# A two-layer graph network on one core: the second batch's preparation regrouped around the first output product

## The chip, the core and the metric

The kernel runs on one core of a Trainium2 chip. The metric is device time in microseconds (us) of one launch. Five engines work side by side, each through its own instructions in program order: TensorE (PE in the profile, with its weight loads as PEld), VectorE (DVE), ScalarE (ACT), GpSimd (POOL) and SyncE (SP), which here issues nearly all DMAs.

## The reference

32 graphs ("batches") of 512 nodes with 512 features pass through two layers. All arithmetic is in fp32.

```python
# layer 0
h = relu(layernorm(x))
agg = (adj @ h) / max(rowsum(adj), 1e-6)
x = x + relu(concat([h, agg], -1) @ W.T)
# layer 1
h = relu(layernorm(x))
q, k = split(h @ Wqk);  v = h @ Wv
w = scale * mask * rowsum(q * (adj @ (k * mask)))
x = x + softmax(w, over the nodes)[:, None] * v
```

## The kernel before

**Products.** Every 512x512 product is computed in seven block products instead of eight, from left and right sums of the operand's quarter blocks. An operand therefore sits in SBUF as seven "slots" of 128 x 512 fp32: the four quarters in slots 0 to 3, and sums of them in slots 4 to 6. `left_sums` and `right_sums` are four VectorE instructions each that fill in slots 4, 6, 5 and rewrite slot 2 (left) or slot 1 (right). `product` (L112) runs through the blocks in the order 1, 2, 6, 5, 7, 3, 4, or with `sooner` 1, 2, 5, 6, 7, 3, 4. Blocks 1, 6, 7 and 4 accumulate in one PSUM tile (`pp`), which ScalarE copies out after each of them (the copies `c11`, `c12`, `c22`), so a block on `pp` can't begin before the copy of the one before it is done.

**Order.** A batch b goes through four products: `layer0_y` (Y: h times the second half of W), `layer0_out` (O: h times the first half, plus adjacency times Y, 14 steps of 8 matmuls), `layer1_tv` (TV, 28 half steps of matmuls, run as 14 steps) and `layer1_u` (U: adjacency times the masked h of layer 1). Y and U have 7 steps of 8 matmuls. The order in time is Y(0), O(0), Y(1), U(0), O(1), TV(0), U(1), Y(2), O(2), and so on. Letters with a batch number are used in this way below.

**Steps.** The program order is written by hand. `run` (L165) advances a product by one step and then emits whatever the `Plan` holds for this step, so an entry `p.at(5, f)` puts f's instructions behind those of step 5 on every engine that they use. A product's copies of a finished block are emitted when the next step begins: in O, `c11` stands at the start of step 2, the DVE work on the first quarter at that of step 4, `c12` at that of step 6, the copy of block 5 at that of step 8, and `c22` at that of step 10. In Y(1), `c11` stands at step 1, the copy of block 5 at 3, `c12` at 4 and `c22` at 5.

**Front work.** While a batch is multiplied, the next ones are prepared:

- `FrontH` (L290) makes h of layer 0: `load` reads x in two halves (8 DMAs of 128 KB), `stats` takes mean and variance of a chunk of 128 rows on VectorE, `variance` forms 1/sqrt on VectorE and GpSimd, `shift` its product with the mean, `write` normalizes a chunk on ScalarE and writes it to DRAM scratch `dhT` (256 KB), `to.read` reads it back with rows and columns exchanged in blocks (4 DMAs of 128 KB a half, tile `shT`), and `turn` transposes a half on VectorE into slots 0, 1 or 2, 3.
- `FrontA` (L317) does this for the adjacency: `load`, `sum` (row sums on ScalarE), `degrees` (VectorE), `write` (scaled by 1/degree on ScalarE, to `daT`), `to.read` (tile `saT`), `turn`.
- `FrontH1` (L357) makes h of layer 1 from the x that O leaves, with `mask` and `masked_sums` for U's right operand and `sh1T` for its transpose; `keep` stores x (1 MB, `dx`).
- `Stream` (L404) reads the seven slots of W's first half ("W1") from DRAM scratch `dw`, 256 KB each, for each O from O(1) on, with four buffers.

In `start` (L778) W1 lies in SBUF as `w1R`, in one half of the tile `tv`, whose other half holds `HT[1]`, the transposed h of batch 1. `w1R` is copied to `dw` for later use, and after O(0) its space becomes Y(1)'s output. The adjacency of batches 0 and 1 uses one tile, `aT`. The half tiles that x and adj are loaded into (tag "n") have two buffers, as have the tiles for the exchanged reads (tag "s").

Of the kernel before, what the change touches and what calls it, by code (L numbers as in the profile page):

```python
# [22 lines left out]
def kernel(  # L23
# [11 lines left out]
    nc = tc.nc  # L35
# [25 lines left out]
    def slots(tag, bufs, name, pool=None):  # L61
        return (pool or big).tile([P, 7, 2, H], F32, tag=tag, bufs=bufs, name=name)
# [19 lines left out]
    def left_sums(s, on=None):  # L82

        return [
            lambda: add(s(4), s(2), s(3), on), lambda: sub(s(6), s(0), s(2), on),
            lambda: sub(s(5), s(4), s(0), on), lambda: sub(s(2), s(1), s(5), on),
        ]
# [7 lines left out]
    def of(t):  # L95
        return lambda i: t[:, i]
# [15 lines left out]
    def product(name, terms, place, finish, seed=False, sooner=False):  # L112

        def m(k, p, first):
            for n, (lt, rt) in enumerate(terms):
                block_product(k, p, lt, rt, first and n == 0)  # L120
                yield

        pp = mm_tile(f"pp_{name}")
        yield from m(1, pp, True)
        if seed:
            pr = seed_tile(f"pr_{name}")
            copy(pr, pp)
            pq = mm_tile(f"pq_{name}")
            yield from m(5, pq, True)
            m5 = block(f"m5_{name}")  # L130
            copy(m5, pq)
            yield from m(6, pp, False)
            c12 = place(0, 1)
            copy(c12, pp)
            yield from m(2, pr, False)
            finish(0, 0, None, pr, None)
        else:
            c11 = place(0, 0)
            copy(c11, pp)
            pr = mm_tile(f"pr_{name}")  # L140
            yield from m(2, pr, True)
            finish(0, 0, c11, pr, c11)
            for k in (5, 6) if sooner else (6, 5):
                if k == 6:
                    yield from m(6, pp, False)
                    c12 = place(0, 1)
                    copy(c12, pp)
                else:
                    pq = mm_tile(f"pq_{name}")
                    yield from m(5, pq, True)  # L150
                    m5 = block(f"m5_{name}")
                    copy(m5, pq)
        yield from m(7, pp, False)
        c22 = place(1, 1)
        copy(c22, pp)
        finish(1, 1, c22, m5, c22)
        yield from m(3, pq, False)
        finish(0, 1, c12, pq, c12)
        yield from m(4, pp, False)
        finish(1, 0, None, pp, None)  # L160

    def right(t):
        return lambda k: t[:, RIGHT[k]]

    def run(phase, n, plan):  # L165

        for i in range(n):
            if phase is not None:
                next(phase)
            for f in plan.get(i, []):  # L170
                f()
        if phase is not None:
            assert next(phase, "end") == "end"
# [79 lines left out]
    def shift(t, a=0, b=C):  # L253
        mv, rstd, nmr = t
        nc.vector.scalar_tensor_tensor(
            nmr[:, a:b], mv[:, a:b, 0], -1.0, rstd[:, a:b], op0=ALU.mult, op1=ALU.mult
        )
# [166 lines left out]
    def into(t):  # L424


        def finish(r, c, o, p, s):
            if s is None:
                copy(t[:, 2 * r + c, :, :], p)
            else:  # L430
                add(o, p, s)

        return (lambda r, c: t[:, 2 * r + c, :, :]), finish

    def layer0_y(b):
        if b not in Y:
            Y[b] = slots("yh", 1, f"y_{b}")
        return product(f"y_{b}", [(HT.get(b, hT), right(w2R))], *into(Y[b]), sooner=b < 2)
# [332 lines left out]
    FH, FA, F1 = {}, {}, {}  # L771
    stream = Stream()
# [5 lines left out]
    def start():  # L778
# [10 lines left out]
        w1R = spread[:, 0:3584].rearrange("p (s b f) -> p s b f", s=7, b=2)  # L789
# [21 lines left out]
        fh = FH[1] = FrontH(1)  # L811
# [36 lines left out]
        def place(d, which, src):  # L848
            nc.scalar.activation(
                mv[:, 2 * (d // 2):2 * (d // 2) + 2, 2 * (d % 2):2 * (d % 2) + 2, which, :],  # L850
                src.rearrange("p (a b f) -> p a b f", a=2, b=2), AF.Copy, scale=1.0 if which else scale,
            )
# [47 lines left out]
        p = Plan()  # L900
# [52 lines left out]
        fb = FA[1] = FrontA(1)  # L953
        p = Plan()
# [1 line left out]
        p.at(0, turn_chunk, Later(rows, 3), 3, "a")  # L956
        p.at(1, keep_chunk, a0, 3, "a")
        p.at(1, fb.load, 0)
        p.at(2, fb.load, 1)
        la = left_sums(of(a0))  # L960
        for k in range(4):
            p.at(2 + k // 2, la[k])
        for c in range(C):
            p.at(2 + c, fh.stats, c)
            p.at(6 + c // 2, fh.write, c)
        p.at(5, variance, fh.t)
        p[6].insert(0, lambda: shift(fh.t))
        p.at(7, lambda: nc.sync.dma_start(out=stream.d.rearrange("s p b f -> p s (b f)"), in_=w1R.rearrange("p s b f -> p s (b f)")))
        p.at(7, mask_order)
        p.at(8, mask_turn)  # L970
        p.at(9, mask_keep)
        p.at(8, fh.to.read, 0)
        p.at(9, fh.to.read, 1)
        for c in range(C):
            p.at(8 + c, lambda c=c: place(c, 1, wvN[:, c, :]))
            p.at(10 + c, fb.sum, c)
        p.at(10, fh.turn, 0)
        p.at(11, fh.turn, 1)
        for k in range(4):
# [1 line left out]
        f = F1[0] = FrontH1(0)  # L981
# [10 lines left out]
        p = Plan()  # L992
# [12 lines left out]
        p.at(2, weights[1])  # L1005
        p.at(3, f.mask, 2)
        p.at(3, f.mask, 3)
        for h in range(2):
            p.at(2 + h, fb.degrees, h)
        for k in range(4):  # L1010
            p.at(4, f.masked_sums, k)
        p.at(4, f.to.read, 0)
        p.at(5, f.to.read, 1)
        p.at(5, fb.write, 0)
        p.at(5, fb.write, 1)
        p.at(5, weights[2])
        p.at(6, weights[3])
        run(layer0_y(1), 7, p)

        fh = FH[2] = FrontH(2)  # L1020
        p = Plan()
        p.at(0, fb.write, 2)
        p.at(0, fb.write, 3)
        p.at(0, f.turn, 0)
        p.at(1, f.turn, 1)
        for n in range(4):
            p.at(0, stream.load)
        p.at(1, fb.to.read, 0)
        p.at(2, fh.load, 0)
        p.at(2, fh.load, 1)  # L1030
        p.at(3, fb.to.read, 1)
        p.at(3, load_x, 1)
        p.at(2, FA[0].factor)
        p.at(2, weights[4])
        r1 = right_sums(of(Y[1]))
        p.at(5, r1[0])
        p.at(6, r1[2])
        for c in range(C):
            p.at(3 + c, fh.stats, c)
        p.at(4, fb.turn, 0)  # L1040
        p.at(6, variance, fh.t)
        run(layer1_u(0), 7, p)
        return weights[5:], mv
# [5 lines left out]
    }  # L1049
    with tc.manual_schedule(engines=engines):  # L1050
        weights, mvR = start()
        post = None
        for i in range(1, B):
            more, last = i + 1 < B, i + 1 == B
            f = F1[i] = FrontH1(i)
            p = Plan()
# [44 lines left out]
            if 1 < i and i + 2 < B:  # L1101
                fh = FH[i + 2]
# [23 lines left out]
            p = Plan()  # L1126
# [19 lines left out]
            if i == 1:  # L1146
# [3 lines left out]
                fh = FH[3]  # L1150
# [29 lines left out]
            p = Plan()  # L1180
# [40 lines left out]
            if more:  # L1221
                p = Plan()
                fb = FA[i + 1]
# [24 lines left out]
        p = Plan()  # L1248
# [11 lines left out]
        p = Plan()  # L1260
# [39 lines left out]
```

## Time and profile before

| | us |
|---|---|
| median of three runs | 2289.23 (2286.17, 2289.23, 2289.88) |
| the profiled execution: its time | 2286.77 |
| the profiled execution: its span, first to last instruction | 2284.8 |
| TensorE busy in the span | 2262.3 (99%) |
| VectorE / ScalarE / GpSimd busy | 1912.4 / 1025.0 / 176.6 |
| DMA traffic | 463.68 MB, mean 203 GB/s |

The start in the same execution, by TensorE's own timeline: the products begin at 24.64 (Y(0)), 39.99 (O(0)), 68.34 (Y(1)), 92.68 (U(0)), 104.77 (O(1)) and 137.27 (TV(0)). A step of 8 matmuls takes 1.73 us from its start to the start of the next when nothing is in its way.

Times in a timeline count from the first instruction. A line there gives start, duration, engine, line of the kernel, instruction, out<-in by the program's tile names, form and count; a bracket gives the engine's idle time before it and what ended it. "SPq" is SyncE's issuing of a DMA, not the transfer.

### The profile page before, as it was taken

The page shows a single profiled execution, that of the slowest core. Times are in us where ns is not written, and L with a number is a line of the kernel's source. Part 1 is how long each engine was busy: PE and PEld are TensorE (multiplying, and loading weights), DVE is VectorE, ACT ScalarE, POOL GpSimd, SP SyncE. Part 2 cuts the span into 40 slices and gives each one's busy share as a digit, 9 for nine tenths or more (in the row PEclk, how much of TensorE's full clock was granted, in tenths as well). Part 3 has the DMA queues.
Part 4 walks back from the last instruction along what each step waited for, and adds up shares of the span by engine and source line. Part 5 has one row for each costly group of instructions (what it writes and reads, how often), then busy time and mean ns, then how long its engine had stood idle before and what let it go on. Part 6 is the DMA issues. An engine that isn't in the chain of part 4 may idle for free.

```text
span 2284.8 us, 32852 instructions
## 1 busy us (share of the span) xinstructions
PE 2262.3 (99%) x10526; PEld 1985.8 (87%) x10526; DVE 1912.4 (84%) x3778; ACT 1025.0 (45%) x1895; POOL 176.6 (8%) x261
## 2 busy tenths in 40 slices
PE   9799999999999999999999999999999999999999
PEld 7688888888888888888888888888888888888888
DVE  6698888888888888888888888888888888888776
ACT  4355344454344544444543454443445434444323
POOL 0000000000000000000011000000000010000000
PEclk9899999999999999999999999999999999999999
DMA  8879777878787877788787878787877877887644
GB/s 183 202 212 245 214 191 209 232 203 209 196 202 219 222 202 209 193 204 233 202 214 199 198 208 231 201 212 187 208 223 216 208 200 197 209 231 204 154 128 107
DMA packets 409900, 463.68 MB, mean 203 GB/s; under 512 B 38112, under 2 KB 271584, under 8 KB 405504
## 3 DMA queue, kind: packets, MB, share of 16 engines
q1 hardware_dynamic: 396512, 426.46, 68.7%
q0 software_dynamic: 8928, 32.51, 8.6%
q10 hardware_dynamic: 4288, 2.62, 0.5%
q8 instruction: 83, 1.36, 0.3%
q14 instruction: 89, 0.73, 0.1%
HBM read 293.93 MB, written 167.51 MB: 202 GB/s over the span
## 4 chain that ended last, share of the span: by engine, by line
PE 94%; DMA 3%; DVE 1%; ACT 0%; issue 0%; SPq 0%; POOL 0%; DVEq 0%; ACTq 0%
PE ptv L470 28%; PE pp_o L103 18%; PE pp_u L103 9%; PE pp_y L103 9%; PE pq_o L103 9%; PE pq_u L103 5%; PE pq_y L103 5%; PE pr_o L103 5%; PE pr_u L103 2%; PE pr_y L103 2%; PE pw L521 1%; DMA w<-dw 1%; DMA mv<-in_L_gnn_Wqk_dram 0%; DMA a<-in_adj_dram 0%; DMA mv<-in_L_gnn_W_dram 0%; DMA dw<-tv 0%
## 5 line engine op out<-in xcount | busy, mean ns | idle before, releaser
L470 PE MATMUL ptv<-mv,h1T 128*128 128x256 f32 x2940 | 639.4, 379 | 0.0
L470 PEld LDWEIGHTS ptv<-mv,h1T 128*128 128x128 f32 x2940 | 558.6, 190 | 75.9
L74 DVE TENSOR_TENSOR tv<-tv 128x256 f32<-128x256 f32 (+1 forms) x645 | 321.5, 510 | 13.2 <-ACT tv L80 1.5
L80 ACT ACTIVATE tv<-ptv 128x512 f32<-128x512 f32 (+1 forms) x360 | 185.0, 541 | 262.9 <-PE ptv L470 261.9
L103 PE MATMUL pp_u<-h1m,aT 128*128 128x256 f32 x1024 | 241.9, 379 | 0.0
L103 PE MATMUL pp_y<-wide 128*128 128x256 f32 x992 | 234.4, 379 | 0.7 <-ACT y L80 0.7
L103 PE MATMUL pp_o<-y,aT 128*128 128x256 f32 x992 | 234.4, 379 | 0.0
L103 PE MATMUL pp_o<-w,wide 128*128 128x256 f32 x960 | 226.8, 379 | 0.0
L103 PEld LDWEIGHTS pp_u<-h1m,aT 128*128 128x128 f32 x1024 | 194.5, 190 | 26.4
L103 PEld LDWEIGHTS pp_y<-wide 128*128 128x128 f32 x992 | 188.3, 190 | 26.6 <-ACT y L80 1.1
L103 PEld LDWEIGHTS pp_o<-y,aT 128*128 128x128 f32 x992 | 188.3, 190 | 25.6
L103 PEld LDWEIGHTS pp_o<-w,wide 128*128 128x128 f32 x960 | 182.4, 190 | 24.8
L80 ACT ACTIVATE o<-pp_o 128x512 f32<-128x512 f32 x96 | 57.3, 597 | 296.0 <-PE pp_o L103 296.0
L80 ACT ACTIVATE y<-pp_y 128x512 f32<-128x512 f32 x124 | 74.0, 597 | 233.8 <-PE pp_y L103 233.8
L74 DVE TENSOR_TENSOR tv<-ptv,tv 128x512 f32<-128x512 f32 x240 | 139.7, 613 | 43.0 <-PE ptv L470 39.2
L77 DVE TENSOR_TENSOR h1T<-h1T 128x512 f32<-128x512 f32 (+1 forms) x189 | 163.3, 878 | 1.3
L80 ACT ACTIVATE xu<-pp_u 128x512 f32<-128x512 f32 x127 | 75.8, 597 | 195.2 <-PE pp_u L103 195.2
L251 POOL TENSOR_TENSOR rstd<-rstd,mhalf 128x2 f32<-128x2 f32 (+1 forms) x97 | 80.0, 825 | 665.4 <-DVE rstd L250 665.4
L103 PE MATMUL pq_u<-h1m,aT 128*128 128x256 f32 x512 | 121.0, 379 | 0.0
L74 DVE TENSOR_TENSOR tv<-ptv,m_tv 128x512 f32<-128x512 f32 (+1 forms) x120 | 72.0, 622 | 56.5 <-PE ptv L470 55.4
L103 PE MATMUL pq_y<-wide 128*128 128x256 f32 x496 | 117.3, 379 | 0.0
L103 PE MATMUL pq_o<-y,aT 128*128 128x256 f32 x496 | 117.2, 379 | 0.0
(167 smaller groups left out, 3321.0 us busy)
## 6 DMA issues: line engine op xcount, KB each, us to landing
w<-dw SPq DMA_DIRECT2D x217, 256.0 KB, 4.2
a<-in_adj_dram SPq DMA_DIRECT2D x256, 128.0 KB, 3.1
dx<-xu SPq DMA_DIRECT2D x32, 1024.0 KB, 4.9
sh1T<-dh1T SPq DMA_DIRECT2D x256, 128.0 KB, 3.4
shT<-dhT SPq DMA_DIRECT2D x248, 128.0 KB, 6.1
daT<-a SPq DMA_DIRECT2D x124, 256.0 KB, 3.1
saT<-daT SPq DMA_DIRECT2D x248, 128.0 KB, 3.4
xu<-in_x_dram SPq DMA_DIRECT2D x124, 256.0 KB, 5.4
```

What stands on the lines that cost most here:

```text
L74: (on or nc.vector).tensor_tensor(o, a, b, op=ALU.add)
L77: (on or nc.vector).tensor_tensor(o, a, b, op=ALU.subtract)
L80: nc.scalar.activation(o, i, AF.Copy)
L103: nc.tensor.matmul(p[:, rc, :], lt[:, LEFT[k], dk, ts(rc, P)], right[:, dk, :], start=first and rc == 0 and dk == 0, stop=True, skip_group ...
L251: nc.gpsimd.tensor_tensor(rstd[:, a:b], rstd[:, a:b], mhalf[:, a:b], op=ALU.pow)
L470: nc.tensor.matmul(banks[n][:, :, ts(i, P)], left[:, LEFT[k], LEFT_IN[j], :], mvR[:, RIGHT[k], RIGHT[j], :, :], start=first and i == 0, st ...
L521: nc.tensor.matmul(banks[n][:, ts(i, P)], left[:, LEFT[k], LEFT_IN[j], :], mvR[:, RIGHT[k], RIGHT[j], which, :], start=first and i == 0, s ...
```

## The change

All of it lies in `start`, in the plans of O(0), Y(1) and U(0).

- In O(0), batch 1's four statistics and their variance move from steps 2 to 5 into step 2, with two of the four sums of `aT` put ahead of them and two behind. The four normalizations and their writes move from steps 6 and 7 to step 5, ahead of the copy `c12`, and the exchanged reads from steps 8 and 9 to step 5.
- The copy of W1 to `dw`, one transfer of 1792 KB behind h's writes, becomes seven of 256 KB: slots 0, 1 and 3 ahead of h's writes (step 2), slots 2, 4, 5 and 6 behind h's reads (step 6).
- Batch 1's adjacency is summed, scaled and written within O(0) (steps 6 to 12) instead of being summed there (10 to 13) and scaled and written in Y(1) and U(0). Its second half is loaded at step 1 instead of 2.
- The mask's work moves by one or two steps.
- In Y(1), the exchanged reads of layer 1's h move one step forward, and the first four loads of W1 slots move here from U(0), behind those reads.
- In U(0), the adjacency's exchanged reads come at steps 0 and 1 (before: 1 and 3), x of batch 2 ("the third x") is loaded behind them (before: between the two), the first adjacency transpose moves from step 4 to 3, ahead of the third x's statistics, which move from steps 3 to 6 into steps 4 and 5.

```diff
@@ O(0)
         p.at(1, fb.load, 0)
-        p.at(2, fb.load, 1)
+        p.at(1, fb.load, 1)
         la = left_sums(of(a0))
-        for k in range(4):
-            p.at(2 + k // 2, la[k])
+
+        def keep_w1(slot):
+            nc.sync.dma_start(out=stream.d[slot], in_=w1R[:, slot])
+
+        for slot in (0, 1, 3):
+            p.at(2, keep_w1, slot)
+        p.at(2, la[0])
+        p.at(2, la[2])
         for c in range(C):
-            p.at(2 + c, fh.stats, c)
-            p.at(6 + c // 2, fh.write, c)
-        p.at(5, variance, fh.t)
-        p[6].insert(0, lambda: shift(fh.t))
-        p.at(7, lambda: nc.sync.dma_start(out=stream.d.rearrange("s p b f -> p s (b f)"), in_=w1R.rearrange("p s b f -> p s (b f)")))
-        p.at(7, mask_order)
-        p.at(8, mask_turn)
-        p.at(9, mask_keep)
-        p.at(8, fh.to.read, 0)
-        p.at(9, fh.to.read, 1)
+            p.at(2, fh.stats, c)
+            p.at(5, fh.write, c)
+        p.at(2, variance, fh.t)
+        p.at(3, la[1])
+        p.at(3, la[3])
+        p[5].insert(0, lambda: shift(fh.t))
+        p.at(5, mask_order)
+        p.at(5, fh.to.read, 0)
+        p.at(5, fh.to.read, 1)
+        for slot in (2, 4, 5, 6):
+            p.at(6, keep_w1, slot)
+        p.at(7, mask_turn)
+        p.at(8, mask_keep)
         for c in range(C):
+            p.at(6 + c, fb.sum, c)
             p.at(8 + c, lambda c=c: place(c, 1, wvN[:, c, :]))
-            p.at(10 + c, fb.sum, c)
+            p.at(9 + c, fb.write, c)
+        for h in range(2):
+            p.at(8 + h, fb.degrees, h)
@@ Y(1)
-        for h in range(2):
-            p.at(2 + h, fb.degrees, h)
+        fh = FH[2] = FrontH(2)
         for k in range(4):
             p.at(4, f.masked_sums, k)
-        p.at(4, f.to.read, 0)
-        p.at(5, f.to.read, 1)
-        p.at(5, fb.write, 0)
-        p.at(5, fb.write, 1)
+        p.at(3, f.to.read, 0)
+        p.at(4, f.to.read, 1)
         p.at(5, weights[2])
         p.at(6, weights[3])
+        for n in range(4):
+            p.at(6, stream.load)
         run(layer0_y(1), 7, p)
@@ U(0)
-        fh = FH[2] = FrontH(2)
         p = Plan()
-        p.at(0, fb.write, 2)
-        p.at(0, fb.write, 3)
         p.at(0, f.turn, 0)
+        p.at(0, fb.to.read, 0)
         p.at(1, f.turn, 1)
-        for n in range(4):
-            p.at(0, stream.load)
-        p.at(1, fb.to.read, 0)
-        p.at(2, fh.load, 0)
+        p.at(1, fb.to.read, 1)
+        p.at(1, fh.load, 0)
         p.at(2, fh.load, 1)
-        p.at(3, fb.to.read, 1)
         p.at(3, load_x, 1)
...
+        p.at(3, fb.turn, 0)
         for c in range(C):
-            p.at(3 + c, fh.stats, c)
-        p.at(4, fb.turn, 0)
+            p.at(4 + c // 2, fh.stats, c)
         p.at(6, variance, fh.t)
         run(layer1_u(0), 7, p)
```

## The prediction, made before the changed kernel was run

> **What bounds the kernel now.** I read the page first: TensorE is busy 99% of the span, and in its timeline no gap stands between 137.27 us and the end, so whatever the change gains or loses, it is the amount by which TV(0) begins earlier or later than 137.27. TensorE's waits, the second view, name what can be won. In this view each line is: who waited, for whom, us in total, times, longest.
>
> ```profile
> PE pp_y L103 <- ACT tv L80: 6.7, 2, 4.9
> PE pp_o L103 <- ACT o L80: 3.6, 2, 2.3
> PE pp_y L103 <- DVE tv L283: 3.0, 1, 3.0
> PE pp_o L103 <- DVE aT L283: 2.2, 1, 2.2
> ```
>
> The four lines make 15.5 us. TensorE's timeline gives each its place; the bracket is the wait.
>
> ```profile
> 68.34 3.68 PE L103 MATMUL pp_y<-wide,tv 128*128 128x256 f32 x8 [3.02 <-DVE tv L283]
> ...
> 80.41 3.78 PE L103 MATMUL pp_y<-wide,tv 128*128 128x256 f32 x8 [4.93 <-ACT tv L80]
> 85.94 3.46 PE L103 MATMUL pp_y<-wide,tv 128*128 128x256 f32 x8 [1.75 <-ACT tv L80]
> ...
> 108.82 3.24 PE L103 MATMUL pp_o<-tv,aT 128*128 128x256 f32 x8 [2.16 <-DVE aT L283]
> ...
> 117.19 1.99 PE L103 MATMUL pp_o<-w,tv 128*128 128x256 f32 x8 [1.24 <-ACT o L80]
> ...
> 133.72 1.99 PE L103 MATMUL pp_o<-w,tv 128*128 128x256 f32 x8 [2.32 <-ACT o L80]
> ```
>
> Eight matmuls take 1.89 us elsewhere, so four blocks behind a wait run at about half speed: 1.8 + 1.9 + 1.6 + 1.35 us more, and 0.5 in the block after 108.82. About 7 us of slow clock and 15.5 of waits, 22.5 us, is the ceiling. Third, who made TensorE wait? The timelines of VectorE, ScalarE and SyncE:
>
> ```profile
> 56.44 0.41 SPq L968 DMA_DIRECT2D dw<-tv  x1
> ...
> 67.05 1.25 DVE L283 STREAM_TRANSPOSE tv<-shT 128x1024 f32<-128x1024 f32 x1 [6.48 <-DMA shT<-dhT]
> 69.54 1.25 DVE L283 STREAM_TRANSPOSE tv<-shT 128x1024 f32<-128x1024 f32 x1 [1.25 <-DMA shT<-dhT]
> ...
> 79.06 0.81 ACT L261 ACTIVATE h<-xu,nmr,rstd 128x512 f32<-128x512 f32 x1 [16.47 <-DVE nmr L255]
> 79.78 0.57 ACT L80 ACTIVATE tv<-pp_y 128x512 f32<-128x512 f32 x1
> ...
> 105.81 0.69 DVE L245 BATCH_NORM_STATS2 st<-n 128x6 f32<-128x512 f32 x1 [6.78 <-DMA n<-in_x_dram]
> ```
>
> W1's copy is issued just ahead of h's reads and takes 7.78 us (chain of waits), so the reads land late and VectorE stands 6.48 us before h's transpose. Behind it in VectorE's order stand layer 1's statistics; ScalarE's normalization waits for their shift (78.90), and Y(1)'s c11 (79.78) stands behind that normalization. In U(0) VectorE stands 6.78 us before the third x, with the adjacency's transpose and the next shift (115.61) behind it. The ends of each wait are thus one VectorE queue.
>
> **The Trainium skill.** "Perfetto Trace Analysis", Tensor Engine Instruction: ScalarE, VectorE and GpSimd are strict FIFO. The rows above agree (79.78 right behind 79.06). "DMA: Bandwidth & Descriptors", Queues, rings and completion order: descriptors are consumed in ring order on each DMA engine. Here SyncE's transfers land in the order of issue (dw at 64.22, the first shT at 64.94 by their last semaphore updates, which give all landings below). "TensorE: Matmul & The Clock Gate", What's actually happening: half clock after an idle window of about 3.4 us, windows free-running. The trace's half-speed stretches (68.4 to 71.9, 78.7 to 88.9, 109.4 to 112.8) agree, but here 2.2 us of wait in a window was enough, and 1.24 was not.
>
> **O(0), step by step.** VectorE begins the first aT sum at 44.39 (backlog, unchanged). Then 2 sums at 0.60 to 45.6; four statistics at 0.82 each (49.85 to 50.67 in the trace; x landed by 40.2) to 48.9; variance; 2 sums to 50.3; the first quarter's two operations 1.32 to 51.58. GpSimd's power takes about 1.2 us from the variance and is ready by then. Shift at 51.58 instead of 52.87: 1.3 us earlier.
> ScalarE takes the four normalizations 0.2 later and then c12, 2.84 after their start (53.07 to 55.91 in the trace): 54.62, done 55.2. This is a cost: c12 used to run at 51.05, and block 7, due at 54.24, now waits until 55.25. Of this 1.0 us the mask's transposes, which took 0.45 of the 2.18 us before step 9, now lie inside the wait, so step 10 is at 58.71 instead of 58.25 and O(0) ends 0.46 later, at 65.6. ScalarE then has no pause: two row sums (0.61 each), block 5's copy 56.34, mask, wv place 0.52, sum, adjacency write 0.66, place, sum, c22 at 59.90 (before 58.51; needed at 62.2). The adjacency work is hidden; if it were not before c22, c22 would be about 1.4 earlier.
> DMA: slots 0, 1, 3 (768 KB) go at 45.7 behind adj (lands 48.8) and are through by about 52, before h's first write (52.6). The writes land at 54.7 to 56.9 (2.1 us after issue, as before). The reads need only their own half's two writes (before: issued 56.95, when two of four had landed), so they are issued from 55.5. Eight exchanged reads cost 0.62 to 0.65 us each (sh1T: 88.50 to 92.83): first half about 60, second about 62.6. The four other slots and the adjacency's writes, 2 MB, are behind them and end by 71, before the next DMA at 73.
> VectorE finishes the second quarter (two operations from c22's end, 60.5) at 61.84. First transpose then, second at 63.1, without waiting. Before: 67.05 and 69.54. TensorE begins Y(1) at 65.6 without a wait (before 68.34).
>
> **Y(1).** From the second transpose to the shift was 9.36 us of VectorE work without a pause (69.54 to 78.90); the same instructions, so shift at 72.46, c11 0.88 later, and step 3 at 73.97. Steps 0 to 2 end at 70.8: a wait of 3.2 remains (was 4.93). From shift to step 4 it is ScalarE's queue of normalizations, masks and copies, 7.04 us (78.90 to 85.94): 79.5. So 6.4 earlier. Step 4 probably runs at half clock again, as in the trace; then U(0) begins at 86.3 instead of 92.68. The degrees leave VectorE (4 x 0.2) without effect.
>
> **U(0) and O(1).** All of layer 1's h moves with the shift, so sh1T lands at 86.4 (before 92.83). Behind it: four W1 slots 4.1 us (96.81 to 100.94) to 90.5, as SyncE issues them right after the reads at 83 to 85; adjacency reads, which wait for the transposes that free their tiles (VectorE, about 87 to 89.6), 2.5 + 2.5 to 95.5; the third x's first half 2.2, at 97.7, second 99.8 (before 105.62, 107.80); x of batch 1 after that. The adjacency's first transpose, at 93.1, is no longer behind the statistics: the wait of 2.16 goes, with its slow clock. What is late next is the shift of the third x: before, from the first statistics (105.81) to it (115.61) 9.80 us without a pause; less the transpose (1.16) 8.64, so 106.4. From there to O(1)'s step 4 it took 1.58 (115.61 to 117.19): 107.98. TensorE could be there at 105.3 (86.3 + 11 x 1.73), so the wait at that place grows from 1.24 to about 2.7. Step 4: 107.98 against 117.19, **9.2 us earlier**. The last wait (2.32, c22 behind a row sum of batch 2's adj, whose load follows the third x's writes) hangs on the same writes and stays; should the clock fall after 2.7 us of wait, the 1.7 us lost are inside it. TV(0) at 128.1.
>
> Sum on the profiled execution: 2286.77 - 9.2 = 2277.6. Its time is 2.46 below the median of the runs, so the median that I forecast is 2289.23 - 9.2 = **2280.0**.
>
> **Unknown costs, from both sides.** The split of the copy: between -0.5 (SyncE is free anyway) and +1.5 (h's reads a little slower beside later transfers; the second transpose has 0.5 us in hand). Half clock: -1.7 to +1.7, as windows are free-running; taken as in the trace. The third x's landing: 95.5 (the rate of the stretch 92.7 to 104.8, 242 GB/s, held throughout) to 101 (180 GB/s, as in 104.8 to 117.2); taken 97.7. The last wait: gone (-2.3) or the same. Together a gain of 5 to 13.
>
> **Rivals.** (1) h's transpose waits for W1's copy all the same, because both lie in one tile: slots 2 to 6 land at about 66.7, the transpose comes 4.85 later than forecast, and all behind it: gain 4.4, 2284.9. Against: at 69.54 the transpose wrote slots of this tile while TensorE read others. (2) Nothing of O(0)'s gain holds, because ScalarE's queue, full from 51.8 to 63.5, makes c12 and c22 later still; U(0)'s order alone gains: third x at 92.83 + 4.1 + 5 + 2.2 = 104.1, step 4 at 114.4, gain 2.8, less 0.5 to 2: 2288. For it: c12 now stands behind four normalizations. Against: each has its measured duration. (3) Slower: the third x, now behind both adjacency reads and the W1 slots, lands so late that VectorE's queue holds O(1). Step 4 is its landing plus 10.3, so it decides from 106.9 on. At 133 GB/s, the rate of a slow slice in the first 250 us, the 2.6 MB ahead of and in it take 19.7 us; from 92.8 (no gain in O(0)) it lands at 112.5, step 4 at 122.8, 5.6 later: 2294.8. For it: two transfers' worth of reads put ahead of it. Against: the daT writes (1 MB) leave this stretch.
>
> **Chances.** Forecast 0.68, (1) 0.10, (2) 0.09, (3) 0.08; 0.05 for more than 13 us. About 0.2%, 4.6 us, is what a measurement of this kernel can tell from no change. Faster: the forecast, a third of (1), and the last: 0.78; same 0.12; slower 0.10. The range 2274 to 2286.5 takes in the forecast's own bounds (2276 to 2284) with the runs' scatter, and (1).
>
> **What would show it.** Right: transposes at about 62 and 63; Y(1)'s step 0 without a wait; a new wait of 1 us at O(0)'s block 7 for an ACT copy; waits of about 3 at Y(1)'s block 6; no wait for the aT transpose; one of 2 to 3 at O(1)'s block 6; TV(0) near 128. Wrong: a wait of VectorE for shT, or the third x's statistics waiting past 102.

## The result, and the profile after

| | before | after |
|---|---|---|
| median, us | 2286.93 (6 runs, 2286.17 to 2289.88) | 2278.66 (6 runs, 2277.19 to 2280.48) |
| profiled execution: time / span | 2286.77 / 2284.8 | 2280.12 / 2278.3 |

The ratio of the runs is 0.9961, with a 95% interval of 0.9949 to 0.9974: about 8 us faster, the forecast said 9.2. The three further runs of the kernel before came out lower than its first three. The profiled execution of the changed kernel lies near the upper end of its runs, so its trace shows a little less gain (6.5 us between the spans) than the medians do. From the start of TV(0) to the end of the span it is 2147.5 us before and 2147.8 after: the whole difference lies ahead of TV(0), as the prediction assumed.

TensorE's waits in the changed kernel, as shown of before (who waited, for whom; total, times, longest):

```profile
PE pp_y L103 <- ACT tv L80: 5.8, 2, 3.1
PE pp_o L103 <- ACT o L80: 5.5, 3, 3.1
```

Both waits for VectorE's transposes (3.0 and 2.2) are gone. One wait for ScalarE in an O was added. TensorE's timeline places them:

```profile
54.79 1.99 PE L103 MATMUL pp_o<-tv,wide 128*128 128x256 f32 x8 [0.74 <-ACT o L80]
...
65.25 1.89 PE L103 MATMUL pp_y<-wide,tv 128*128 128x256 f32 x8
...
73.32 2.40 PE L103 MATMUL pp_y<-wide,tv 128*128 128x256 f32 x8 [2.72 <-ACT tv L80]
78.84 3.78 PE L103 MATMUL pp_y<-wide,tv 128*128 128x256 f32 x8 [3.12 <-ACT tv L80]
82.41 3.18 PE L103 MATMUL pq_y<-wide,tv 128*128 128x256 f32 x8
...
107.94 2.00 PE L103 MATMUL pp_o<-w,tv 128*128 128x256 f32 x8 [1.63 <-ACT o L80]
...
125.21 3.08 PE L103 MATMUL pp_o<-w,tv 128*128 128x256 f32 x8 [3.12 <-ACT o L80]
128.08 2.54 PE L103 MATMUL pp_o<-tv,aT 128*128 128x256 f32 x8
130.46 9.88 PE L470 MATMUL ptv<-mv,h1T 128*128 128x256 f32 x45
```

Y(1) begins without a wait (65.25, before 68.34), and TV(0) at 130.46 instead of 137.27. In this execution O(0) already began 0.72 earlier (39.27, before 39.99), where nothing was changed, so that 6.1 of TV(0)'s 6.8 us come from the change; comparisons with the forecast below add this 0.72. SyncE's timeline shows the new order of the transfers, VectorE's what it brought:

```profile
44.98 1.47 SPq L963 DMA_DIRECT2D dw<-tv  x3
52.16 2.44 SPq L309 DMA_DIRECT2D dhT<-mv  x4
54.97 4.06 SPq L212 DMA_DIRECT2D shT<-dhT  x8
59.09 2.29 SPq L963 DMA_DIRECT2D dw<-tv  x4
```
```profile
61.32 2.36 DVE L283 STREAM_TRANSPOSE tv<-shT 128x1024 f32<-128x1024 f32 x2
...
71.80 0.13 DVE L255 SCALAR_TENSOR_TENSOR nmr<-mv,rstd 128x2 f32<-128x2 f32 x1
...
98.14 0.69 DVE L245 BATCH_NORM_STATS2 st<-n 128x6 f32<-128x512 f32 x1 [3.48 <-DMA n<-in_x_dram]
...
106.40 0.16 DVE L255 SCALAR_TENSOR_TENSOR nmr<-mv,rstd 128x4 f32<-128x4 f32 x1
```

h's reads are issued in one go, with no transfer of W1 between them and h's writes. The two transposes stand back to back and wait for nothing (before: 6.48 and 1.25 us).

### The profile page after: what moved, and what is told of

Read it like the earlier page. It is cut to its first block, busy times and chain, and to the rows that moved or that the text cites. A ratio compares the mean times of both kernels' runs of the same rounds, so it can differ in the third digit from the quotient of the medians.

```text
span 2278.3 us, 32859 instructions
## 1 busy us (share of the span) xinstructions
PE 2260.0 (99%) x10526; PEld 1985.7 (87%) x10526; DVE 1913.3 (84%) x3778; ACT 1025.2 (45%) x1895; POOL 177.6 (8%) x261
## 4 chain that ended last, share of the span: by engine, by line
PE 94%; DMA 3%; DVE 2%; SPq 0%; ACT 0%; issue 0%; DVEq 0%; ACTq 0%
PE ptv L470 28%; PE pp_o L103 18%; PE pp_u L103 9%; PE pp_y L103 9%; PE pq_o L103 9%; PE pq_u L103 5%; PE pr_o L103 5%; PE pq_y L103 5%; PE pr_u L103 2%; PE pr_y L103 2%; PE pw L521 1%; DMA shT<-dhT 1%; DMA mv<-in_L_gnn_Wqk_dram 0%; DMA mv<-in_L_gnn_W_dram 0%; SPq L212 0%; DVE st L245 0%
```

## The experiments

The theory on trial: the start is one VectorE queue. It begins with h's transpose (held by W1's copy in the rings), passes through layer 1's statistics, and ends with the third x's shift, on which ScalarE's copy, TensorE's block 6 of O(1) and, through batch 2's adjacency, its last wait hang. Its rival: the gain comes from taking the adjacency's traffic out of the fullest stretch of DMA. All ratios are to the kernel before.

| kernel | median us | ratio, 95% interval |
|---|---|---|
| h part alone | 2281.92 | 0.9972 (0.9963 to 0.9981) |
| adjacency part alone | 2284.40 | 0.9987 (0.9980 to 0.9993) |
| changed, W1 whole | 2282.84 | 0.9979 (0.9971 to 0.9988) |
| before, W1 behind | 2282.27 | 0.9979 (0.9969 to 0.9988) |
| changed, c12 first | 2278.17 | 0.9959 (0.9946 to 0.9971) |
| changed, third x between | 2273.88 | 0.9943 (0.9930 to 0.9955) |
| third x early | 2271.52 | 0.9933 (0.9920 to 0.9945) |
| the same, c11 first | 2271.72 | 0.9931 (0.9918 to 0.9945) |
| the same, W1 loads behind | 2267.25 | 0.9909 (0.9896 to 0.9923) |

**The two halves of the change.** First the kernel before with only h's steps and the split copy; then only the adjacency's sums and writes in O(0) with the new order of Y(1) and U(0).

```diff
# h part alone: the changed kernel with these taken back
-            p.at(6 + c, fb.sum, c)
-            p.at(9 + c, fb.write, c)
-            p.at(8 + h, fb.degrees, h)
+            p.at(10 + c, fb.sum, c)
# ... and Y(1), U(0) as in the kernel before
```

> The kernel before with the h part alone: statistics, normalizations and reads of batch 1's h moved as in the change, W1's copy in seven transfers. The adjacency and the third x stay as before. Theory (one VectorE queue, started by h's transpose, ended by the third x's shift): transposes at about 61.5 and 62.5 us, Y(1)'s block 7 at about 79, as in the changed kernel. In U(0) the adjacency's writes lie ahead of the third x again; counted from the last landing of the exchanged reads of layer 1's h (12.8 us in the kernel before, 12.4 in the changed one) the third x's first half lands at 98.4, but 9.8 us of VectorE work follow until its shift instead of 8.3, so O(1)'s block 6 begins about 2 us later than in the changed kernel: 2281 us, 6 below before. Rival (the adjacency's traffic taken out of the full stretch is the gain): little gained, 2285 or more.

> The kernel before with the adjacency part alone: sums, scaling and writes of batch 1's adjacency in O(0), the reordered Y(1) and U(0). h and W1's single copy stay as before. Theory: transposes of h at 67 and 69.5 us or somewhat later, Y(1) as before, its block 7 at about 86; the adjacency's transpose no longer delays O(1)'s second step, the third x lands 12.4 us after layer 1's exchanged reads, at 105.2, and O(1)'s block 6 begins at about 115 instead of 117.2: 2285 us, 2 below before. The two parts together make the change's gain (6 + 2). Rival: 2280, most of the gain lies here.

Measured: 2281.92 and 2284.40, against 2287.78 of the kernel before measured beside them, 5.9 and 3.4 us. They add up to 9.2, the whole change against the same 2287.78 (9.1); neither is an alternative account of the other. In the h part alone the transposes came at 61.49 and 63.24 and Y(1)'s block 7 at 79.64. The old order of U(0) kept its own wait: the adjacency's transpose, behind the third x's statistics (99.48), cost TensorE 1.93 us, and block 6 of O(1) began at 110.85. In the adjacency part alone Y(1) is as before (block 7 at 85.79), and block 6 of O(1) begins at 114.26 instead of 117.19. The rival would have put most of the gain there, and as built it is the smaller part. That doesn't settle the rival: the adjacency part also contains the third x's new place, which a later experiment shows to be a loss of 4.8 us. Without that loss the adjacency part brings 8.0 us on top of the h part (2281.92 against the 2273.88 of "changed, third x between"), more than the h part brings alone. Which of its steps brings them (the adjacency's writes taken out of Y(1) and U(0), layer 1's reads and the W1 loads put earlier, the adjacency's transpose put ahead of the statistics) was not separated.

**W1's copy.** Its place is tested from both sides: the changed kernel with the one big transfer again between h's writes and reads, and the kernel before with that one line moved behind the reads.

```diff
# changed, W1 whole
-            p.at(2, keep_w1, slot)          # slots 0, 1, 3
-            p.at(6, keep_w1, slot)          # slots 2, 4, 5, 6
+        p.at(5, ...)                        # the one transfer of before, ahead of fh.to.read
# before, W1 behind
-        p.at(7, ...)                        # the one transfer
         p.at(9, fh.to.read, 1)
+        p.at(9, ...)
```

> The changed kernel with W1's copy in one transfer of 1792 KB again, between h's writes and h's reads. Theory: the reads stand behind it in the rings; 1792 KB at the 375 GB/s that it had before are about 4.8 us, so the transposes come at about 65.5 and 67.5 instead of 61.3 and 62.5, the shift of layer 1 at 77 instead of 71.8, and all behind it is 5 us later: 2283.5. Rival (the place of the statistics and normalizations brings the gain, the split is incidental): unchanged, 2278.7.

> The kernel before with one line moved: W1's single copy of 1792 KB behind h's reads instead of ahead of them. Theory (the copy's place in the rings is what held h): the reads land from 58 us on, the transposes come at about 62 and 64.5 instead of 67.05 and 69.54, and what follows is 5 us earlier up to U(0), where the reads of the adjacency and the third x take over as in the kernel before: about 2282.5, near the 2281.9 of the whole h part. Rival (moving the statistics and normalizations forward is what counts): 2286 or more.

VectorE's timeline, first of the changed kernel with W1 whole, then of the kernel before with W1 behind:

```profile
65.27 1.25 DVE L283 STREAM_TRANSPOSE tv<-shT 128x1024 f32<-128x1024 f32 x1 [4.06 <-DMA shT<-dhT]
67.78 1.25 DVE L283 STREAM_TRANSPOSE tv<-shT 128x1024 f32<-128x1024 f32 x1 [1.26 <-DMA shT<-dhT]
...
77.14 0.13 DVE L255 SCALAR_TENSOR_TENSOR nmr<-mv,rstd 128x2 f32<-128x2 f32 x1
```
```profile
60.04 1.25 DVE L283 STREAM_TRANSPOSE tv<-shT 128x1024 f32<-128x1024 f32 x1
62.70 1.25 DVE L283 STREAM_TRANSPOSE tv<-shT 128x1024 f32<-128x1024 f32 x1 [1.42 <-DMA shT<-dhT]
...
72.06 0.13 DVE L255 SCALAR_TENSOR_TENSOR nmr<-mv,rstd 128x2 f32<-128x2 f32 x1
```

With the copy back in front of the reads, the transposes wait again and layer 1's shift comes 5.3 us later than in the changed kernel, close to the 4.8 that the expectation took for the copy's bytes; the median loses 4.2. With nothing but the one line moved, the kernel before reaches 2282.27, as much as the whole h part (2281.92). So the moved statistics and normalizations, and the copy's cut into seven, brought nothing that can be told beside what the order of two transfers brings.

**The wait that the change added.** Normalizations, writes and reads go to step 6, so that ScalarE does c12 first.

```diff
-            p.at(5, fh.write, c)
+            p.at(6, fh.write, c)
-        p[5].insert(0, lambda: shift(fh.t))
+        p.at(5, lambda: shift(fh.t))
-        p.at(5, fh.to.read, 0)
-        p.at(5, fh.to.read, 1)
+        p.at(6, fh.to.read, 0)
+        p.at(6, fh.to.read, 1)
```

> The changed kernel with the four normalizations, h's writes and reads at step 6, behind the copy c12, not ahead of it. Theory: c12 runs at once and TensorE's wait at O(0)'s block 7 (0.74 us in the changed kernel) goes, so Y(1) begins about 0.5 earlier; but the second transpose of h already begins within 0.3 us of its data, which come no earlier, so what follows it stays within 0.3 us: 2278.4, no change that can be told. Rival (that wait is a price paid in full): 2277.9 or less.

2278.17, and the wait of 0.74 is gone from TensorE's list. The second transpose now waits 0.17 us for its data (62.36), so the queue behind it begins no earlier. The difference of 0.5 us to the changed kernel is inside what these runs can tell: the wait cost little or nothing, and nothing more is shown.

**The third x.** Only the adjacency's second read goes behind the third x's load again.

```diff
         p.at(1, f.turn, 1)
-        p.at(1, fb.to.read, 1)
         p.at(1, fh.load, 0)
         p.at(2, fh.load, 1)
+        p.at(3, fb.to.read, 1)
         p.at(3, load_x, 1)
```

> The changed kernel with the adjacency's second exchanged read behind the third x's load again (steps 1, 2, then 3). Theory (the third x's landing sets its shift, and this O(1)'s block 6 and the last wait): the third x lands about 2.4 us earlier, at 95.6 and 98; the shift at 104 instead of 106.4; TensorE's wait at O(1)'s block 6 (1.63 us) goes, and the last wait begins from writes that are 2.4 us earlier: 2276.5, 1.5 to 2.4 us below the changed kernel. So the third x behind the adjacency's reads would be a cost of the change. Rival (the adjacency's second transpose is the limit): no change or slower by up to 2 us.

VectorE's, then TensorE's timeline of this kernel:

```profile
94.47 0.69 DVE L245 BATCH_NORM_STATS2 st<-n 128x6 f32<-128x512 f32 x1 [0.76 <-DMA n<-in_x_dram]
...
102.73 0.15 DVE L255 SCALAR_TENSOR_TENSOR nmr<-mv,rstd 128x4 f32<-128x4 f32 x1
```
```profile
105.20 1.89 PE L103 MATMUL pp_o<-w,tv 128*128 128x256 f32 x8
...
120.88 1.99 PE L103 MATMUL pp_o<-w,tv 128*128 128x256 f32 x8 [1.69 <-ACT o L80]
124.43 15.92 PE L470 MATMUL ptv<-mv,h1T 128*128 128x256 f32 x73
```

2273.88, 4.8 us below the changed kernel, twice the upper end of what was expected. This execution began 0.85 earlier at Y(1) (64.40). Without that the shift comes 2.8 earlier, block 6 has no wait and begins 1.9 earlier, the last wait is 1.69 instead of 3.12, and the two steps behind it run at full clock, which is another 1.7. The expectation had named the first two, at 1.5 to 2.4 us together, and not the clock. So "the third x behind adj's reads", a part of the change, is a cost.

**The versions that follow from it.** The stretch from the adjacency's last write to layer 1's first write (67.5 to 72.8 us) has no transfers. There the third x is loaded; its statistics go into Y(1), its shift and writes into U(0), and batch 2's adjacency is loaded two to three steps earlier.

```diff
# only the lines put in; x of batch 1 is besides loaded one step earlier in U(0)
# Y(1)
+        p.at(0, fh.load, 0)
+        p.at(0, fh.load, 1)
+            p.at(4, fh.stats, c)
+        p.at(4, variance, fh.t)
# U(0)
+        p.at(2, shift, fh.t)
+            p.at(3 + c, fh.write, c)
# O(1)
+                p.at(2, fa.load, 0)
+                p.at(3, fa.load, 1)
```

> The changed kernel with the third x loaded at Y(1)'s step 0, where the transfers stand idle between the adjacency's last write (67.5 us) and layer 1's first (72.8); its statistics follow in Y(1), its shift and writes in U(0), and batch 2's adjacency is loaded at O(1)'s steps 2 and 3. Theory: O(1)'s block 6 no longer waits (1.63 us), the last wait (3.12 us and some 1.8 of slow clock) goes because the adjacency comes about 8 us earlier; U(0) begins as before or up to 0.5 later: O(1) runs without a wait, 24.2 us from 99.2 to 123.4 instead of 130.5, 7 us below the changed kernel: 2271.7. Rival (the traffic only collides elsewhere: layer 1's exchanged reads or the adjacency's land later): less than 3 us gained.

```profile
PE pp_y L103 <- ACT tv L80: 5.6, 2, 2.9
```

That is the only line of TensorE's waits in this kernel that begins behind Y(0): O(1) runs without one, TV(0) begins at 123.39, the median is 2271.52. These moves were made together, so what each is worth is not shown. Next, ScalarE's order in Y(1): layer 1's normalizations behind c11, the later ones and the masks behind c12 and c22.

```diff
-        p.at(0, write, 0)
+        p.at(1, write, 0)
-        p.at(2, write, 2)
-        p.at(2, write, 3)
+        p.at(4, write, 2)
+        p.at(4, f.mask, 0)
+        p.at(4, write, 3)
+            p.at(5, f.mask, c)              # c = 1 to 3
# the first four W1 loads between the adjacency's two reads; layer 1's exchanged reads and
# masked sums one step later, the third x's statistics one earlier
```

> The kernel with the third x early, and besides in Y(1) the normalizations of layer 1's h behind c11, two of them and the masks behind c12 and c22, and the first W1 loads between the adjacency's two reads. Theory: c11 no longer waits for the shift at 71.8, so block 6 begins at 70.4 without a wait; block 7 waits for c12 behind two normalizations, until about 74.5 instead of 78.8; U(0) begins at about 80 to 81 instead of 87.2. The adjacency's reads then are the next limit, at O(1)'s second step. 2266, 5 to 6 below the kernel with the third x early alone. Rival (layer 1's exchanged reads, which hang on the shift and stay where they are, hold U(0)'s followers): 2270 or more.

2271.72, a miss: nothing gained. VectorE's timeline, then TensorE's and ScalarE's:

```profile
98.36 1.25 DVE L283 STREAM_TRANSPOSE aT<-saT 128x1024 f32<-128x1024 f32 x1 [3.52 <-DMA saT<-daT]
...
115.23 0.16 DVE L337 TENSOR_SCALAR deg<-deg 128x2 f32<-128x2 f32 x1
```
```profile
74.77 3.46 PE L103 MATMUL pp_y<-wide,tv 128*128 128x256 f32 x8 [2.19 <-ACT tv L80]
...
81.74 1.89 PE L103 MATMUL pp_u<-h1m,aT 128*128 128x256 f32 x8
...
117.56 1.99 PE L103 MATMUL pp_o<-w,tv 128*128 128x256 f32 x8 [2.84 <-ACT o L80]
```
```profile
115.69 0.72 ACT L346 ACTIVATE a<-a,rdeg 128x512 f32<-128x512 f32 x1 [5.36 <-DVE rdeg L338]
...
116.93 0.57 ACT L80 ACTIVATE o<-pp_o 128x512 f32<-128x512 f32 x1
```

U(0) does begin 5.4 us earlier than in the changed kernel (81.74 against 87.15), and as much earlier than with the third x early (87.12). TV(0) begins only 2.3 earlier than with the third x early (121.11 against 123.39), and the medians show no gain at all: much is given back at O(1)'s end. The median is the one that the rival gave, but not for the rival's reason: TensorE waits for nothing from U(0)'s start to this last wait. The W1 loads put between the adjacency's reads hold the second read, VectorE waits 3.52 us, the degrees behind it in its queue come at 115.23, and ScalarE's scaling of batch 2's adjacency (115.69), which needs them, stands ahead of c22 (116.93). One edit tests it: three of the four W1 loads behind the second read.

> The kernel with c11 first, with three of its first four W1 loads moved behind the adjacency's second exchanged read (one stays between the two). Theory (there the second transpose of the adjacency waited 3.52 us for its data behind four W1 slots, and VectorE's queue behind it, with the degrees of batch 2's adjacency, held ScalarE's c22 and so TensorE for 2.84 us): the read lands about 3 us earlier, VectorE's queue moves by as much, the 2.84 go, TV(0) begins at about 118.3 instead of 121.1: 2269, 2.5 below it and below the kernel with the third x early. Rival (the adjacency's load itself is what c22's queue waits for): unchanged, 2271.7.

```profile
PE pp_y L103 <- ACT tv L80: 2.2, 1, 2.2
...
PE pq_u L103 <- ACT m_u L80: 1.0, 1, 1.0
...
PE pp_o L103 <- ACT o L80: 0.6, 1, 0.6
```
```profile
94.94 1.25 DVE L283 STREAM_TRANSPOSE aT<-saT 128x1024 f32<-128x1024 f32 x1 [0.50 <-DMA saT<-daT]
...
111.82 0.16 DVE L337 TENSOR_SCALAR deg<-deg 128x2 f32<-128x2 f32 x1
```
```profile
74.55 1.99 PE L103 MATMUL pp_y<-wide,tv 128*128 128x256 f32 x8 [2.18 <-ACT tv L80]
```

2267.25, 20.7 below the kernel before measured beside it and 11.4 below the changed kernel. VectorE's queue is 3.4 us earlier, the 2.84 are gone (the 0.6 is O(0)'s block 7, at 54.83) and TV(0) begins at 117.70. The gain over the kernel without this edit is 4.5 us where 2.5 were expected. Of it, 1.9 stands in U(0)'s start already (79.83 against 81.74), ahead of the edit: there the same wait at Y(1)'s block 7 did not bring the clock down. It is the fastest kernel of the study.

## Why the prediction was right, and which sizes were off

Forecast, and in brackets what the changed kernel's trace shows with the 0.72 added:

- O(0): h's shift at 51.58 (51.85), block 7 held until 55.25 (55.51), transposes at 61.84 and 63.1 (62.04 and 63.20). The reads were taken as being held by W1's copy ahead of them in the rings; the two experiments on its place show that its being issued ahead of them is what held them.
- Y(1): layer 1's shift at 72.46 (72.52), block 6 at 73.97 (74.04), block 7 at 79.5 (79.56). VectorE's 9.36 us and ScalarE's 7.04 were carried over whole from the old trace, and they held.
- U(0) at 86.3 (87.87): off by 1.6. For block 7 and what follows it one slow block was counted, as in the trace of before; two came (78.84 and 82.41).
- The third x's statistics at about 97.9 (98.86), O(1)'s block 6 at 107.98 (108.66). VectorE's timeline and the chain of waits of the changed kernel show how the slow clock reached the third x:

```profile
85.63 0.69 DVE L74 TENSOR_TENSOR tv<-pq_y,tv 128x512 f32<-128x512 f32 x1 [0.52 <-PE pq_y L103]
```
```profile
86.25 1.21 DVE mv L77
87.45 1.22 DVE h1T L288 x2
88.69 0.32 SPq L212
...
93.94 4.07 DMA n<-in_x_dram
98.14 0.70 DVE st L245
```

  Y(1)'s slow blocks 7 and 3 let VectorE finish late (it waits 0.52 us for block 3), so its transposes of layer 1's h, which free the tiles for the adjacency's reads, began about 1.1 us later than the 87 forecast, and the third x is queued behind those reads.
- The term that was mis-sized is the last wait, of which the forecast says that it "hangs on the same writes and stays" at 2.32, and that a fall of the clock at block 6 would be made up inside it. Block 6's wait was 1.63 instead of the 2.7 forecast, and the clock didn't fall there. The last wait was 3.12, and the clock fell behind it: the steps at 125.21 and 128.08 took 5.62 instead of the 3.88 of before (133.72 and 135.55). Why the last wait grew by 0.8 isn't settled: ScalarE's row sum ahead of c22 came 17.55 us behind the third x's shift, 16.85 before. Of the 1.6 above, block 6's wait had absorbed all but 0.7; with 0.8 of wait and 1.7 of slow clock this makes TV(0) 131.2 instead of 128.1 in this execution. Other executions did better: the medians are 8.3 apart, close to 9.2.
- Luck has a part in the 2280.0 that was forecast, 1.3 above the measured 2278.66. The gain was sized 0.9 too large, but it was taken from the first three runs of the kernel before, whose median lies 2.3 above that of all six.
- A slip in the chances: the three parts named for "faster" make 0.76, not 0.78.
- The rivals: that h's transpose would wait for W1's copy because both lie in one tile fell (61.32 without a wait, while slots 2, 4, 5 and 6 were still on their way: the last was issued at 60.5, and these copies take 3.8 to 4.5 us). That ScalarE's queue in O(0) would eat the gain fell too: it held TensorE for the 0.74 us above. The third x's landing did rule the end of the start, the rival's mechanism, but at 98 and not beyond its limit of 106.9.
- What the forecast did not see: that putting the third x behind the adjacency's second read was itself a loss of 4.8 us. It priced the landing at this place and never the other order.

## What to carry to other kernels

Where an engine in strict order waits for a read-back, look first at which transfers were issued ahead of that read and are not needed soon: moving one line brought as much as the whole h part. When such a wait goes, follow the same engine's queue to its next wait and ask what is ahead of that transfer, since one read put ahead of the third x cost 4.8 us, and the changed kernel without it is 13.9 us faster than the kernel before. An idle stretch of the DMA engines beside a full one is a place for the next load.

## What the hardware showed that was not expected

Waits of about the same length did and did not bring TensorE down to half clock. Behind 1.93 us (h part alone) the next eight matmuls took 2.82 and behind 2.16 (before) 3.24. Behind 2.32 (before, last wait), 2.36 (adjacency part alone, block 6 of O(1)), 2.41 (W1 behind, last wait) and 2.84 (c11 first, last wait) they took 1.99, as they do behind 1.24 (before), at full clock. The forecast took 2.2 us of wait as enough; the 2.32 of the same trace was not. The closest pair is Y(1)'s block 7: 3.46 behind 2.19 us with c11 first, 1.99 behind 2.18 in the fastest kernel.

"TensorE: Matmul & The Clock Gate", What's actually happening, in the Trainium skill, has free-running windows of about 3.4 us, which would fit such scatter; no run here shows the windows themselves. The waits of 1.93 and 2.16 are shorter than the whole idle window that it names for a fall, and there the measurement decides. Each of these two was followed by some 1.8 us lost over two steps (2.82 and 2.79, 3.24 and 2.37, instead of 1.89 each). So a wait of 2 us cost 2 to 4 us in these traces, with the clock's fall or without it. Whether that differs between executions of one kernel is not shown, as each kernel has one trace.
